# Expert gathers issued by a tile budget of 20 buffers instead of three parts ahead

## The chip, the cores and the metric

The kernel runs on one core of a Trainium2 chip. Its time is device microseconds for one execution. The engines are PE (matrix products), DVE (vector work), ACT (activations), Pool (here almost only the issue of indirect DMAs, that is, gathers and scatters by a list of rows) and SP (issue of plain DMAs). Each engine runs its own queue of instructions in order and waits on semaphores for the others. A DMA is issued by an engine and lands later; whoever needs its data waits for its landing.

## The reference, cut to what matters

A graph layer on 12500 nodes with 256 features, followed by a mixture of 64 experts, a norm over the nodes, a residual and a norm over the features. The part that the change touches is the mixture (shortened):

```python
logits = x @ Wg + bg
vals, idx = jax.lax.top_k(logits, TOP_K)          # two experts for each node
gates = jax.nn.softmax(vals, axis=-1)
...
h1 = gelu(einsum('ecd,edh->ech', h, w1) + b1)     # h: the tokens of each expert, 256 -> 512
h2 = einsum('ech,ehd->ecd', h1, w2) + b2          # 512 -> 256
y = zeros((N, D)).at[tok_s].add(g_s[:, None] * y_s)
```

So each node goes to two of 64 experts, its two results are weighted and added to the node's row. All data are float32.

## The kernel before, in words

The first two thirds of the time (to about 2620 us) sum the edges into the nodes, make each node's row `x2_d` (256 features and two gates), pick its two experts and number the tokens of each expert. The last 140 us are the two norms. Between them lies the stage of the experts.

There the 64 experts are ordered by their number of tokens, and `TOKENS` gives each place in this order its room (in units of 16 tokens). The room of one expert is cut into one or two **parts** of at most four **tiles** of 128 tokens; there are 73 parts with 219 tiles. Of 16 pairs of experts the last, partly filled tiles ("tails") share one product buffer (`pair_of_outputs`). For part q the loop does, in this order:

- `hidden(q)`: first layer on PE (L1960), gelu on ACT (L1964);
- `begin(q + AHEAD)` with `AHEAD = 3`: for a new expert, register loads that tell its number, three small copies by DVE of its token lists (`sort_slots`, L2118 and L2120), its weights by SP (`load`, L1884, 1026 KB, four buffers); then one gather by Pool for each tile of part q + 3 (`gather`, L1931) into one of 16 buffers `xg`;
- `turned(q + 1)`: PE turns the gathered tiles of the next part (L1947), DVE copies them to SBUF (L1951);
- `gates(q)` on DVE (L1975), `outputs(q)`: second layer on PE (L1983), bias and gate on DVE into one of ten buffers `yo` (L1987, L1988), and one scatter by Pool for each tile, which adds the rows to the nodes in `z_d` (`add_to_nodes`, L1993).

For the second part of a pair, `begin` comes between the scatters of the two tails.

PE and DVE follow the order that is written out here. For Pool, `in_order` ties every gather and scatter to those before it, so Pool's order is that of the code, too: gathers of part q + 3, scatters of part q, gathers of part q + 4, and so on. `landed` adds a real wait: since two experts may add to the same node, the scatters of one group (an expert) are only issued when those of the group before have landed in memory. Twelve tiles whose products were made long before ("early tiles", `add_early`, L1562) are added within this stage: `adds_at` puts such a scatter into the middle of the gathers of twelve of the parts, and it is a group of its own. From part 6 on, SP also loads `x` back (L2151) into the place of the early tiles.

Of the kernel before, what the change touches and what calls it, by code (L numbers as in the profile page):

```python
# [8 lines left out]
F32 = mybir.dt.float32  # L9
# [10 lines left out]
P = 128  # L20
# [3 lines left out]
E = 64  # L24
# [109 lines left out]
RPE = CAP // P  # L134
# [4 lines left out]
D2 = D + 2  # L139
# [5 lines left out]
def gnn_moe_kernel(  # L145
# [1726 lines left out]
    with ExitStack() as stack:  # L1872
# [3 lines left out]
        ps1 = stack.enter_context(tc.tile_pool(name="x_ps1", bufs=1, space=PSUM))  # L1876
        ps2 = stack.enter_context(tc.tile_pool(name="x_ps2", bufs=2, space=PSUM))

        REGS, YO, COLS = 4, 10, RPE - 1
        assert max(TOKENS) * TU <= COLS * P  # L1880

        def load(e):
            w = wp.tile([P, WROW], F32, name="w")
            nc.sync.dma_start(w, wpack[bass.ds(e, 1)].rearrange("a p f -> p (a f)"))  # L1884
# [35 lines left out]
        def gather(at, m, q=None):  # L1920

            xg = []
            for k in range(0, m, P):
                if k // P == -(-m // P) // 2 and q in adds_at:
                    st = add_early(adds_at[q], taken_at)
                    landed(st, f"early{adds_at[q]}")
                    in_order(st)
                r = max(WHOLE, min(P, m - k))
                k //= P
                g = two.tile([P, D2], F32, name="xg", bufs=16)  # L1930
                i = GP.indirect_dma_start(  # L1931
                    out=g[:r],
                    out_offset=None,
                    in_=x2_d,
                    in_offset=bass.IndirectOffsetOnAxis(ap=at[:r, 0, k : k + 1], axis=0),
                )
                in_order(i)
                xg.append(g[:r])
            return xg
# [139 lines left out]
        adds_at.update({large[(2 * i + 1) * len(large) // (2 * n)]: AT_ONCE + i for i in range(n)})  # L2079
        xg, given = {}, {}  # L2080

        def begin(q):
            i, b, m = parts[q]
            if i not in given:
                if i not in columns_of:
                    n = 1
                    at = order.index(i)
                    while n < REGS and order[at : at + n + 1] == [*range(i, i + n + 1)]:
                        n += 1
                    _, regs = nc.values_load_multi_w_load_instructions(  # L2090
                        exp_row[0:1, i : i + n],
                        engines=[SP],
                        min_val=0,
                        max_val=E - 1,
                        skip_runtime_bounds_check_because="exp_row is an order of the experts",
                    )
                    _, columns = nc.values_load_multi_w_load_instructions(
                        exp8_row[0:1, i : i + n],
                        engines=[DVE],
                        min_val=0,  # L2100
                        max_val=(E - 1) * RPE + 1,
                        skip_runtime_bounds_check_because="exp8_row is an order of the experts",
                    )
                    for k in range(n):
                        columns_of[i + k], reg_of[i + k] = columns[k], regs[k]
                sort_slots(i, 0)
                if q >= AHEAD:
                    sort_slots(i, 1)
                given[i] = load(reg_of[i])
            xg[q] = gather(table(q), m, q)  # L2110

        columns_of, reg_of = {}, {}

        def sort_slots(i, which):

            to = slice(i * RPE, i * RPE + COLS)
            of = bass.ds(columns_of[i], COLS)
            V.tensor_copy(sorted_[:, which, to], slot[:, which, of])  # L2118
# [14 lines left out]
        kept = {}  # L2133
        snd_sorted = one.tile([P, NSLOT], F32)
        with tc.manual_schedule(engines={mybir.EngineType.PE, DVE}):
            for q in range(AHEAD):
                begin(q)
            V.scalar_tensor_tensor(free, node, 0.0, spread, op0=ALU.is_equal, op1=ALU.mult)
            V.tensor_tensor(slot[:, 1], free, slot[:, 0], op=ALU.add)
            for i in sorted({parts[q][0] for q in range(AHEAD)}):  # L2140
                sort_slots(i, 1)
            xT = turned(0)
            for q, (i, b, m) in enumerate(parts):
# [6 lines left out]
                    r = rows(t0)  # L2150
                    nc.sync.dma_start(xs[:r, t0 : t0 + n], part_of(x, t0, n))  # L2151
# [246 lines left out]
```

## Time and profile before

| | us |
|---|---|
| median of three runs | 3597.57 |
| lowest and highest of them | 3569.35 and 3601.11 |
| the profiled execution's own time | 3578.71 |
| its span, first to last instruction | 3576.9 |

| engine | busy us (share of the span) |
|---|---|
| PE | 2494.7 (70%) |
| DVE | 1797.0 (50%) |
| ACT | 826.2 (23%) |
| Pool | 2186.7 (61%) |

The granted clock of PE is 0.82 of full speed in the mean over the span. In a timeline, each line has the start (us from the span's start), the duration, engine, line of the code, operation, what it writes and reads, a count, and in brackets how long the engine had been idle before it and what ended this. That releaser is inferred: where the engine named had long been done, it was another, often a DMA. A gather or scatter is busy on Pool only while it is issued; its landing is later. The table has shares over stages with different limits; what the change is worth is to be read from the experts' stage.

### The profile page before, as it was taken

What the parts mean: (1) busy time and instruction counts of PE and PEld (TensorE: products, weight loads), DVE (VectorE), ACT (ScalarE), POOL (GpSimd) and SP (SyncE); (2) the same over time, 40 slices, a digit from 0 to 9 for tenths busy, and PEclk for the clock granted to TensorE, in tenths of its full rate; (3) what the DMA queues carried; (4) which work ended last, traced back from release to release, by engine and by line L of the source; (5) the groups of instructions that cost most, each with busy time, mean ns of one, the idle gap of its engine ahead of it and who ended that gap; (6) DMA issues with size and microseconds to landing.
All of it is one profiled execution on the core that took longest, in us unless ns stands there. A gap on an engine that the chain in (4) does not pass through costs nothing. (4 is left out here: it accounts for less than half of the span.)

```text
span 3576.9 us, 40976 instructions
## 1 busy us (share of the span) xinstructions
PE 2494.7 (70%) x12046; PEld 1898.2 (53%) x12121; DVE 1797.0 (50%) x7367; ACT 826.2 (23%) x2028; POOL 2186.7 (61%) x2169
## 2 busy tenths in 40 slices
PE   2626066566666667676676666578769999999966
PEld 1515033455555545555555455456547767767756
DVE  2829554255455555655455444356643333334347
ACT  1515301122112122121222112122112211211246
POOL 6270777666666666666665666666547777777621
PEclk6657567788787878788788787788889999999988
DMA  7370853455455554555554544445466667667764
GB/s 258 109 235 4 304 191 110 144 146 152 130 144 143 147 142 139 146 140 162 162 162 145 162 152 137 138 144 179 132 171 148 162 150 193 161 173 183 174 168 144
DMA packets 319779, 562.31 MB, mean 157 GB/s; under 512 B 47850, under 2 KB 236366, under 8 KB 308798
## 3 DMA queue, kind: packets, MB, share of 16 engines
q0 software_dynamic: 119456, 266.90, 29.4%
q1 hardware_dynamic: 186555, 279.83, 24.5%
q10 hardware_dynamic: 13539, 12.90, 1.2%
q8 instruction: 99, 1.62, 0.2%
q14 instruction: 130, 1.06, 0.1%
HBM read 455.41 MB, written 105.12 MB: 157 GB/s over the span
## 5 line engine op out<-in xcount | busy, mean ns | idle before, releaser
L962 POOL DMA_INDIRECT ring<-h_d,src_col x1416 | 1364.4, 964 | 748.1 <-issue 385.4
L976 PE MATMUL p<-ring,o 128*128 128x258 f32 x2832 | 899.3, 447 | 175.0 <-DMA ring<-h_d,src_col 97.1
L976 PEld LDWEIGHTS p<-ring,o 128*128 128x128 f32 x2832 | 594.7, 223 | 337.3 <-issue 148.0
L954 DVE TENSOR_SCALAR o<-lane,rel 128x128 f32<-128x128 f32 x1416 | 356.4, 298 | 328.6 <-remote 163.8
L1993 POOL DMA_INDIRECT z_d<-yo,tables x219 | 340.5, 1555 | 146.2 <-issue 48.9
L1983 PE MATMUL yp<-w,h 128*128 128x256 f32 (+7 forms) x1928 | 381.2, 392 | 9.4 <-DVE yo L1987 8.4
L1960 PE MATMUL hp<-xT,w 128*128 128x384 f32 (+22 forms) x1168 | 350.5, 454 | 2.0 <-DVE xT L1951 1.3
L1983 PEld LDWEIGHTS yp<-w,h 128*128 128x128 f32 (+7 forms) x1928 | 296.3, 174 | 71.3 <-issue 17.2
L1964 ACT ACTIVATE h<-hp,w 128x384 f32<-128x384 f32 (+21 forms) x292 | 159.1, 546 | 622.8 <-PE hp L1960 513.7
L1960 PEld LDWEIGHTS hp<-xT,w 128*128 128x128 f32 x1168 | 218.6, 192 | 112.3 <-issue 49.6
L1931 POOL DMA_INDIRECT xg<-x_d,tables x219 | 215.3, 983 | 77.9 <-issue 52.1
L1951 DVE COPY xT<-xtp 128x768 f32<-128x768 f32 (+20 forms) x73 | 63.6, 871 | 329.6 <-PE xtp L1947 295.5
L1755 ACT ACTIVATE again<-again,factor 128x256 f32<-128x256 f32 x180 | 82.4, 502 | 634.2 <-issue 364.3
L309 POOL DMA_INDIRECT early<-in_x,src_col x140 | 149.8, 1070 | 113.4 <-DMA early_d<-early 60.8
L1051 PE MATMUL q<-ident,s 128*128 128x128 f32 x236 | 58.8, 339 | 200.7 <-DVE tables L1738 72.8
L1010 ACT COPY s<-p 128x258 f32<-128x258 f32 x118 | 44.0, 373 | 636.8 <-remote 274.1
L1730 PE MATMUL q<-r_out,tables 128*128 128x98 f32 x360 | 70.1, 327 | 160.0 <-DVE tables L1738 59.0
L591 PE MATMUL deg<-o_hi,o_lo 128*128 128x98 bf16 x1254 | 105.8, 255 | 102.8 <-issue 66.0
L1987 DVE TENSOR_TENSOR yo<-yp,bb 128x256 f32<-128x256 f32 (+6 forms) x219 | 92.9, 424 | 162.5 <-PE yp L1983 132.4
L589 ACT ACTIVATE s_lo<-lane_b,nb 128x128 bf16<-128x128 bf16 x396 | 122.1, 388 | 201.6 <-PE deg_s L593 96.0
L1730 PEld LDWEIGHTS q<-r_out,tables 128*128 128x128 f32 x360 | 65.7, 238 | 177.3 <-issue 74.4
L1051 PEld LDWEIGHTS q<-ident,s 128*128 128x128 f32 x236 | 35.2, 171 | 234.4 <-DVE tables L1738 79.5
(428 smaller groups left out, 3853.0 us busy)
## 6 DMA issues: line engine op xcount, KB each, us to landing
w<-in_wpack SPq DMA_DIRECT2D x64, 1026.0 KB
again<-early_d SPq DMA_DIRECT2D x90, 256.0 KB
ring<-h_d,src_col POOLq DMA_INDIRECT x1416
acc<-in_wpack SPq DMA_DIRECT2D x20, 1026.0 KB
early_d<-early SPq DMA_DIRECT2D x70, 256.0 KB
tables<-h_d SPq DMA_DIRECT2D x104, 128.0 KB
acc<-acc_d SPq DMA_DIRECT2D x14, 896.0 KB
acc<-in_x SPq DMA_DIRECT2D x12, 1024.0 KB
```

The costliest lines, as they stand in the source:

```text
L309: GP.indirect_dma_start(out=t[:, c % 2], out_offset=None, in_=x, in_offset=bass.IndirectOffsetOnAxis(ap=src_col[:, MC + c : MC + c + 1], a ...
L589: S.activation(s_lo[:, i], lane_b, AF.Sign, bias=nb[:, k - k0, i : i + 1])
L591: T.matmul(deg, o_lo[:, i], o_hi[:, i], start=c + i == 0, stop=False)
L954: o_last[u] = V.tensor_scalar(o_of[u][:, j], lane, rel[:, c : c + 1], None, op0=ALU.is_equal)
L962: i = GP.indirect_dma_start(out=r[:, k, :D], out_offset=None, in_=h_d, in_offset=bass.IndirectOffsetOnAxis(ap=src_col[:, c : c + 1], axis=0),)
L976: i = T.matmul(p_of[g], o_of[v][:, n], r[:, k], start=j == 0, stop=j == GR - 1)
L1730: T.matmul(p_r[:, i], wide[:, i * P : (i + 1) * P], r_out, start=True, stop=True)
L1931: i = GP.indirect_dma_start(out=g[:r], out_offset=None, in_=x2_d, in_offset=bass.IndirectOffsetOnAxis(ap=at[:r, 0, k : k + 1], axis=0),)
L1960: T.matmul(hp[:, :m], w1[:, c, j * P : (j + 1) * P], xT[:, c, :m], start=c == 0, stop=c == 1,)
L1964: S.activation(h1[:, j, :m], hp[:, :m], AF.Gelu, bias=w[:, 2 * H + 4 * D + j : 2 * H + 4 * D + j + 1],)
L1983: T.matmul(yp, h1[:, j, a : a + r], w2[:, j], start=j == 0, stop=j == 3)
L1993: st = GP.indirect_dma_start(out=z_d, out_offset=bass.IndirectOffsetOnAxis(ap=at[:r, 1, k : k + 1], axis=0), in_=yo, in_offset=None, compu ...
```

## The change

The buffers `xg` go from 16 to 20. `begin(q)` no longer stands for one part. It keeps two counters: parts whose weights were asked for (`loaded`), still up to part q + 3, and parts whose gathers were issued (`fetched`). It issues the gathers of further parts, at most two parts in one call, as long as the tiles from part q to the new one are at most 20. The register loads (`names`) and the copies of the token lists come with whichever of the two is first. The call before the loop issues three parts, as before. The early tiles stay in the middle of the gathers of the same parts, and so are issued when these are. At the end no gathers are left from the call for part 67 on.

```diff
-        REGS, YO, COLS = 4, 10, RPE - 1
+        REGS, YO, COLS, XG = 4, 10, RPE - 1, 20
...
-                g = two.tile([P, D2], F32, name="xg", bufs=16)
+                g = two.tile([P, D2], F32, name="xg", bufs=XG)
...
+        tiles_of = [-(-m // P) for _, _, m in parts]
...
-        def begin(q):
-            i, b, m = parts[q]
-            if i not in given:
...
-                sort_slots(i, 0)
-                if q >= AHEAD:
-                    sort_slots(i, 1)
-                given[i] = load(reg_of[i])
-            xg[q] = gather(table(q), m, q)
+        loaded, fetched = [0], [0]
+
+        def names(i):
+            if i in columns_of:
+                return
...
+        def begin(q, which=1):
+
+            to = min(q + AHEAD, len(parts) - 1)
+            most = fetched[0] + 2 if which else AHEAD
+            while True:
+                p = fetched[0]
+                if loaded[0] <= to and (loaded[0] <= p or p >= most):
+                    i = parts[loaded[0]][0]
+                    names(i)
+                    if i not in given:
+                        given[i] = load(reg_of[i])
+                    loaded[0] += 1
+                elif p < min(most, len(parts)) and sum(tiles_of[max(q, 0) : p + 1]) <= XG:
+                    i, b, m = parts[p]
+                    names(i)
+                    if i not in laid:
+                        sort_slots(i, 0)
+                        if which:
+                            sort_slots(i, 1)
+                        laid.append(i)
+                    xg[p] = gather(table(p), m, p)
+                    fetched[0] += 1
+                elif loaded[0] > to:
+                    break
+                else:
+                    most = p
...
-            for q in range(AHEAD):
-                begin(q)
+            begin(-1, 0)
...
-                if q not in pair_at and q + AHEAD < len(parts):
-                    begin(q + AHEAD)
+                if q not in pair_at:
+                    begin(q)
...
                     rest = pair_of_outputs([kept.pop(pair_at[q]), mine])
-                    begin(q + AHEAD)
+                    begin(q)
```

More of the change, by code (lines that the diff above doesn't have):

```diff
@@ L2080, in gnn_moe_kernel @@
         xg, given = {}, {}
-        def begin(q):
-            i, b, m = parts[q]
-            if i not in given:
[L2085 to L2105, printed above, removed]
-                sort_slots(i, 0)
-                if q >= AHEAD:
-                    sort_slots(i, 1)
-                given[i] = load(reg_of[i])
-            xg[q] = gather(table(q), m, q)
@@ new lines, in gnn_moe_kernel @@
+        loaded, fetched = [0], [0]
+        def names(i):
+            if i in columns_of:
+                return
+            n = 1
+            at = order.index(i)
+            while n < REGS and order[at : at + n + 1] == [*range(i, i + n + 1)]:
+                n += 1
+            _, regs = nc.values_load_multi_w_load_instructions(
+                exp_row[0:1, i : i + n],
+                engines=[SP],
+                min_val=0,
+                max_val=E - 1,
+                skip_runtime_bounds_check_because="exp_row is an order of the experts",
+            )
+            _, columns = nc.values_load_multi_w_load_instructions(
+                exp8_row[0:1, i : i + n],
+                engines=[DVE],
+                min_val=0,
+                max_val=(E - 1) * RPE + 1,
+                skip_runtime_bounds_check_because="exp8_row is an order of the experts",
+            )
+            for k in range(n):
+                columns_of[i + k], reg_of[i + k] = columns[k], regs[k]
@@ L2112, in gnn_moe_kernel @@
+        laid = []
         columns_of, reg_of = {}, {}
@@ L2135, in gnn_moe_kernel @@
         with tc.manual_schedule(engines={mybir.EngineType.PE, DVE}):
-            for q in range(AHEAD):
-                begin(q)
+            begin(-1, 0)
             V.scalar_tensor_tensor(free, node, 0.0, spread, op0=ALU.is_equal, op1=ALU.mult)
             V.tensor_tensor(slot[:, 1], free, slot[:, 0], op=ALU.add)
-            for i in sorted({parts[q][0] for q in range(AHEAD)}):
+            for i in laid:
                 sort_slots(i, 1)
```

## The prediction

> **What bounds the kernel now.** I read the page first, then the stage of the experts (about 2630 to 3438 us of the span) by stretches, then who waited for whom, and last the timelines of Pool and PE side by side. The page, groups by line (busy us, mean ns of one, then idle before it and what ended it):
>
> ```profile
> span 3576.9 us, 40976 instructions
> ...
> L1993 POOL DMA_INDIRECT z_d<-yo,tables x219 | 340.5, 1555 | 146.2 <-issue 48.9 <-DVE yo L1988 36.1 <-DMA z_d<-yo,tables 25.2
> ...
> L1931 POOL DMA_INDIRECT xg<-x_d,tables x219 | 215.3, 983 | 77.9 <-issue 52.1 <-PE yp L1983 12.2 <-PE hp L1960 7.9
> ```
>
> One stretch of the stage (us, then busy us of PE, PEld, DVE, ACT, POOL) and PE's largest wait for data there:
>
> ```profile
> 3000.00:3100.00 100.00, 97.71 (x444) 72.99 (x443) 38.94 (x120) 20.28 (x36) 74.84 (x59) 0.98 0.74 176
> ```
>
> ```profile
> PE xtp L1947 <- DMA xg<-x_d,tables: 19.0, 18, 2.4
> ```
>
> PE looks like the bound, at 97.7 of 100, and it loses 19.0 us in 18 waits for gathered tokens. That is all the change can reach on PE directly. But why is a gather late that is asked for three parts (some 33 us) early? Pool, then PE, around one such wait:
>
> ```profile
> 3160.38 1.11 POOL L1931 DMA_INDIRECT xg<-x_d,tables  x1 [0.30 <-issue]
> ...
> 3164.48 0.92 POOL L1931 DMA_INDIRECT xg<-x_d,tables  x1 [0.31 <-issue]
> ```
>
> ```profile
> 3147.14 5.38 PE L1983 MATMUL yp<-w,h 128*128 128x256 f32 x24
> ...
> 3162.34 4.68 PE L1960 MATMUL hp<-xT,w 128*128 128x336 f32 x16
> 3168.51 0.44 PE L1947 MATMUL xtp<-ident,xg 128*128 128x128 f32 x2 [1.49 <-DMA xg<-x_d,tables]
> ...
> 3172.09 8.04 PE L1983 MATMUL yp<-w,h 128*128 128x256 f32 x24
> ```
>
> The four gathers of part 50 are issued between 3160.38 and 3165.40, and PE, done with part 49's first layer, wants the first at 3167.02 (3162.34 + 4.68). So Pool runs almost two parts behind the place where the code asks. Its order is fixed (scatters of a part, gathers, scatters of the next), so a late scatter makes a late gather. A scatter's own wait, late in the stage (DVE, then Pool):
>
> ```profile
> 3341.08 0.35 DVE L1988 TENSOR_SCALAR yo<-yo,gate 128x256 f32<-128x256 f32 x1
> ```
>
> ```profile
> 3344.68 1.59 POOL L1993 DMA_INDIRECT z_d<-yo,tables  x1 [0.30 <-DVE yo L1987]
> ...
> 3353.10 1.62 POOL L1993 DMA_INDIRECT z_d<-yo,tables  x1 [2.95 <-DVE gate L1975]
> ```
>
> The tile scattered at 3353.10 was ready at 3341.43, and the DVE named as releaser had long been done. What came last is the landing of the scatter that ended at 3346.27: an expert's scatters wait until those of the group before (an expert, or an early tile) have landed. From 2690 on no scatter in the trace starts within a microsecond of its tile. **Pool's chain of scatters, landings and gathers sets the pace**, and PE's waits are its echo. At the end:
>
> ```profile
> 3381.14 1.55 POOL L1993 DMA_INDIRECT z_d<-yo,tables  x1 [0.30 <-issue]
> ...
> 3387.80 1.62 POOL L1993 DMA_INDIRECT z_d<-yo,tables  x1 [1.24 <-issue]
> ...
> 3391.61 1.57 POOL L1993 DMA_INDIRECT z_d<-yo,tables  x1 [0.30 <-issue]
> 3393.49 1.02 POOL L1931 DMA_INDIRECT xg<-x_d,tables  x1 [0.30 <-PE hp L1960]
> ...
> 3401.33 1.62 POOL L1993 DMA_INDIRECT z_d<-yo,tables  x1 [4.29 <-DVE yo L1987]
> ...
> 3418.16 1.59 POOL L1993 DMA_INDIRECT z_d<-yo,tables  x1 [3.00 <-DVE gate L1975]
> ...
> 3426.67 1.55 POOL L1993 DMA_INDIRECT z_d<-yo,tables  x1 [3.19 <-DMA z_d<-yo,tables]
> ...
> 3434.97 1.55 POOL L1993 DMA_INDIRECT z_d<-yo,tables  x1 [3.04 <-DMA z_d<-yo,tables]
> 3436.83 1.42 POOL L1993 DMA_INDIRECT z_d<-yo,tables  x1 [0.30 <-issue]
> ```
>
> ```profile
> 3389.67 0.33 SPq L1884 DMA_DIRECT2D w<-in_wpack  x1
> ```
>
> With no gather behind it and no weights on the way, a landing takes 3.0 to 3.2 us. The one from 3393.18 to 3401.33 took 8.15, with a weight load issued at 3389.67. A scatter costs 1.57 + 0.30 = 1.87 us of Pool, a gather 0.98 + 0.30 = 1.28. So two gathers fit into a quiet landing for nothing, and six into the loaded one.
>
> **The change, part by part.** Its own work is the same: 219 gathers, 219 scatters, 64 loads asked for at the same places against PE, and the same copies of token lists by DVE (one of three lines of them):
>
> ```profile
> L2118 DVE COPY tables<-tables 128x7 int32 x128 | 20.5, 189 | 9.8 <-issue 5.1
> ```
>
> They come a few parts earlier; DVE is idle for 61 of 100 us, and if PE had to wait for the copies of one more expert in the first calls, that is three times 0.19 us. Four more token buffers are only space. The change adds no wait of its own: a gather is asked for when its buffers are free by the count of 20. The early tiles go out sooner, so SP's loads of x that follow them don't start later. What changes is Pool's order. I wrote both orders out from the rule of `begin` over the list of 73 parts.
>
> *First term: the start.* Pool then still waits for PE:
>
> ```profile
> 2640.87 0.96 POOL L1931 DMA_INDIRECT xg<-x_d,tables  x1 [0.51 <-DVE tables L2118]
> ...
> 2649.09 1.65 POOL L1993 DMA_INDIRECT z_d<-yo,tables  x1 [6.06 <-DVE yo L1988]
> 2651.05 1.42 POOL L1993 DMA_INDIRECT z_d<-yo,tables  x1 [0.30 <-issue]
> ...
> 2660.37 1.62 POOL L1993 DMA_INDIRECT z_d<-yo,tables  x1 [4.06 <-DVE yo L1988]
> ...
> 2672.41 1.62 POOL L1993 DMA_INDIRECT z_d<-yo,tables  x1 [2.27 <-DVE yo L1988]
> ...
> 2678.88 1.46 POOL L1993 DMA_INDIRECT z_d<-yo,tables  x1 [2.96 <-DVE yo L1988]
> ...
> 2685.55 1.57 POOL L1562 DMA_INDIRECT z_d<-acc,taken_at  x1 [3.81 <-issue]
> ...
> 2690.04 1.40 POOL L1993 DMA_INDIRECT z_d<-yo,tables  x1 [0.30 <-issue]
> ```
>
> ```profile
> 2649.95 0.33 SPq L1884 DMA_DIRECT2D w<-in_wpack  x1
> ...
> 2650.97 0.39 SPq L2151 DMA_DIRECT2D acc<-in_x  x1
> ```
>
> 19.2 us of idle (6.06 + 4.06 + 2.27 + 2.96 + 3.81). After: five gathers from 2640.87 end at 2647.3, under the first wait. Scatters of part 0 end at 2652.47 as before. Three gathers to 2656.3, then the first early tile, which must see part 0 landed: 3.0 at best, 8.15 at worst; with both loads above on the way I take 6.0, so it is issued from 2658.5 to 2660.1, two gathers to 2662.6, landed at 2663.0. Four scatters to 2670.5, four gathers to 2675.6, two scatters to 2679.3, the kept tail to 2681.1, five gathers to 2687.5. The pair's second tail starts at 2687.8 instead of 2690.04, with nine more gathers behind it (parts 7 to 10). **-2.2 - 9 x 1.28 = -13.7 us** (-16.7 at 3.0, -11.5 at 8.15).
>
> *Second term: landings laid bare.* From there on before has 73 changes of group: 3 with no gather between, 4 with one, 29 with two, 37 with more. After has 75 (two early tiles now split an expert's scatters): 10 with none, 4 with one, 28 with two, 33 with more. None occurs where `begin` finds its 20 tiles full (parts 11, 13, 35, 38) and from part 67 on, where no gathers are left. At the quiet 3.0 us a bare change costs 3.0, one with two gathers 0.44, one with more only its 0.30 of issue: 7 x 3.0 - 0.44 - 4 x 0.30 = **+19.4 us**. Loaded, each of the seven costs up to 8.15 instead of 3.0, +36 more.
>
> *Third term: the end.* With PE no longer held up by gathers, its last weight loads fall earlier against Pool, and the changes into parts 67 and 68 should be quiet. Before, the second took 8.15 and the first 5.10 (from 3382.69 to 3387.80), where three gathers alone make 3 x 1.28 + 0.30 = 4.14: -4.0 - 1.0 = **-5 us**, bounds 0 and -5.
>
> The scatter's landing is also in the Trainium skill, DMA: Bandwidth & Descriptors, section "Anatomy of one DMA — SWDGE (gpsimd) path": about 2.0 us fixed, mostly the write's receipt, plus the bytes at 436 GB/s. For 128 KB that makes an estimate of 2.3 us, under the measured 3.0. By it the seven bare changes would cost 16 us rather than 21, and the sum would be about 5 us lower. It speaks against the change all the same: the wait is a latency that only other issues hide.
>
> **Sum:** -13.7 + 19.4 - 5 = +0.7 us. The profiled execution took 3578.71 us (1.8 of it around the span), so 3579.4 by that account. The median of the runs, 3597.57, lies 18.9 us above it, and the three runs spread over 32 us: I forecast 3598. A difference under 1% (36 us) can hardly be told from none here.
>
> **The rivals.** *PE is the bound (faster).* If landings fall quiet after the shift, Pool keeps up and PE's 19.0 us go. More goes with them: the 24 matmuls at 3172.09, behind such a stall, took 8.04 us against 5.38 for the same 24 undisturbed. The Trainium skill, TensorE: Matmul & The Clock Gate, section "HAM oscillation — how this bites in real kernels", says the same, that waits for data let the array's clock fall. The 18 waits come some three to a part, six stalls; at 2.7 us at most for each, I take 11 of 16: 19 + 11 = 30 less, of which Pool's tail behind PE may keep 5: -25, so 3573. Against it: Pool's lag never closes between 2690 and the end. It decides if Pool's waits for landings shrink by over 25 us.
>
> *Bare landings under load (slower).* Running freely, PE goes ahead until its ten output buffers are full; then its steps, and with them the weight loads, are tied to Pool's landings, and loads fall on the bare changes again. From half of the seven at 8.15 (+18) and no gain at the end (+5) it is +24; with all seven +42. I price it between, +32: 3630.
>
> *Nothing moves.* Were Pool's queue so late that the earlier request changes no issue time, the time stays 3598. Against it: Pool's 19.2 us of idle at the start, which only earlier requests fill.
>
> **How the numbers follow.** Forecast 0.52 (3580 to 3615), PE-bound 0.22, bare and loaded 0.20, nothing moved 0.06. The range takes in both rivals and some of the runs' spread: 3562 to 3634. Faster by over 1% needs the first rival at its full 30 us and luck besides: 0.07. Slower by over 1% is the upper half of the second: 0.15. Within 1%: 0.78.
>
> **What would show it.** First term: gathers of parts 3 and 4 back to back before the first scatter, and little Pool idle before 2690. Forecast as a whole: PE's waits for gathers gone, Pool's lag behind PE larger (over 20 us late in the stage), waits of PE or DVE for output buffers in their place, the last scatter near 3438. Second term: gaps of 3 us on Pool into parts 11, 13, 35, 38 and 67 to 72. It is wrong if scatters start right behind their tiles after 2700 (then PE is the bound), or if those gaps are 5 to 8 us.

## The result and the profile after

The changed kernel is slower by 1.2%: a median of 3631.74 us (six runs, 3625.17 to 3641.24) against 3595.26 us for the kernel before (six runs, 3569.22 to 3601.11), a ratio of 1.0119 with a 95% interval of 1.0086 to 1.0152. The forecast of 3598 us and "no change" was wrong. The time lies just inside the range and almost on the rival "bare landings under load" (3630 us). Medians here and in the table below are over all executions, while the ratios and their intervals leave out those in a slower state of the chip.

The page and Pool's groups of the profiled execution of after (it took 3638.54 us; columns: busy us, mean ns of one, then idle just before and what ended most of it):

```profile
span 3636.4 us, 40984 instructions
```

```profile
L1993 POOL DMA_INDIRECT z_d<-yo,tables x219 | 339.4, 1550 | 183.3 <-issue 52.9 <-DVE yo L1987 43.9 <-DVE yo L1988 30.7
L1931 POOL DMA_INDIRECT xg<-x_d,tables x219 | 213.3, 974 | 77.4 <-issue 53.9 <-PE yp L1983 9.1 <-PE hp L1960 8.2
```

Pool's busy time is that of before. The idle time ahead of the scatters went from 146.2 to 183.3 us: 37.1 more, as much as the whole loss of 36.5. Ahead of the gathers it stayed (77.9 and 77.4). PE's waits in the stage of the experts of after (us, count, longest):

```profile
PE yp L1983 <- DVE yo L1987: 39.6, 21, 4.2
PE hp L1960 <- DMA w<-in_wpack: 6.5, 1, 6.5
PE xtp L1947 <- DMA xg<-x_d,tables: 2.0, 3, 1.1
```

PE's 19.0 us of waits for gathered tokens went down to 2.0, which is what more gathers ahead can do. In their place stand 39.6 us of waits for DVE, and DVE waits for free output buffers. The waits of all engines in that stage of after have the row

```profile
DVE yo L1987 <- DMA z_d<-yo,tables: 104.1, 44, 10.3
```

and before the row was

```profile
DVE yo L1987 <- DMA z_d<-yo,tables: 1.7, 2, 0.9
```

A buffer `yo` is free when its scatter has landed, so PE is now held by Pool's chain from behind. The stretch in which PE was busy for 97.71 us has 92.12:

```profile
3000.00:3100.00 100.00, 92.12 (x417) 67.72 (x416) 36.21 (x112) 18.26 (x33) 69.69 (x57) 0.97 0.70 174
```

For a ledger I followed Pool's 450 instructions of the stage, from its first gather to the end of its last scatter (2629.35 to 3438.25 us before, 2652.61 to 3497.72 after), and put each idle time over 0.5 us down to the tile, where the scatter started as soon as its tile was ready, or else to the landing of the group before.

| us of Pool in the stage | before | after | difference |
|---|---|---|---|
| busy | 575.0 | 572.1 | -2.9 |
| gaps of issue | 125.0 | 123.5 | -1.5 |
| waiting for the tile | 15.4 | 8.1 | -7.3 |
| waiting for a landing | 93.1 | 141.4 | +48.3 |
| the stage | 808.9 | 845.1 | +36.2 |

The stage of after starts 23.3 us later in this one execution. That happens ahead of the changed code; in other runs on such chips it starts between 2607 and 2660 us, with the changed kernel and without.

By the number of gathers that stand between two groups, the idle time at the change of group (whatever ended it) is:

| gathers between | before: changes, us | after: changes, us |
|---|---|---|
| none ("bare") | 3, 9.2 | 10, 47.2 |
| one | 5, 12.5 | 4, 12.2 |
| two | 30, 35.6 | 29, 45.2 |
| three and more | 38, 52.3 | 35, 48.1 |

Seven of the ten bare changes of after stood in before as well, with gathers beside them, and cost 7.7 us there. So at the same ten places (parts 11, 13, 35, 38 and 67 to 72) the idle time rose from 16.9 to 47.2 us, by 30.3; the other 12.8 of the 43.1 us lie at the covered changes. In waits for landings alone it is 31.3 of the 48.3 us at the ten places (15.9 to 47.2) and 17.0 at the covered ones (77.2 to 94.2). Two of the bare changes, into parts 11 and 13, on Pool of after (start, duration, then idle in brackets):

```profile
2784.07 1.46 POOL L1993 DMA_INDIRECT z_d<-yo,tables  x1 [0.30 <-DVE gate L1975]
2793.31 1.56 POOL L1993 DMA_INDIRECT z_d<-yo,tables  x1 [7.78 <-DVE gate L1975]
...
2805.24 0.91 POOL L1931 DMA_INDIRECT xg<-x_d,tables  x1 [0.30 <-issue]
...
2808.39 1.46 POOL L1993 DMA_INDIRECT z_d<-yo,tables  x1 [0.31 <-issue]
2815.13 1.40 POOL L1993 DMA_INDIRECT z_d<-yo,tables  x1 [5.27 <-DVE yo L1988]
```

and SP's loads of weights beside them:

```profile
2784.82 0.33 SPq L1884 DMA_DIRECT2D w<-in_wpack  x1
...
2804.38 0.33 SPq L1884 DMA_DIRECT2D w<-in_wpack  x1
```

A load is issued 0.75 us after the scatter of 2784.07 starts, and the landing is waited for during 7.78 us, with nothing of Pool's to do. Then six gathers go out in a row to 2806.15, between scatters of one expert, where nothing has to land: the cover is there, but at the wrong place. The end of the stage in after, Pool and then SP:

```profile
3443.47 1.57 POOL L1993 DMA_INDIRECT z_d<-yo,tables  x1 [0.30 <-issue]
3450.40 1.55 POOL L1993 DMA_INDIRECT z_d<-yo,tables  x1 [5.36 <-DVE yo L1988]
...
3458.67 1.55 POOL L1993 DMA_INDIRECT z_d<-yo,tables  x1 [3.00 <-DVE gate L1975]
...
3476.88 1.55 POOL L1993 DMA_INDIRECT z_d<-yo,tables  x1 [4.66 <-DMA z_d<-yo,tables]
...
3486.10 1.55 POOL L1993 DMA_INDIRECT z_d<-yo,tables  x1 [3.96 <-issue]
```

```profile
3439.98 0.33 SPq L1884 DMA_DIRECT2D w<-in_wpack  x1
```

The change into part 67 has a load under way (3439.98) and takes 5.36; the one into part 68 has none and takes 3.00. Those into 70 and 71 take 4.66 and 3.96 without any load of weights; what slows them no row shows.

### The profile page after: what moved, and what is told of

It is laid out like the page before. It is cut to its first block, busy times and chain, and to the rows that moved or that the text cites. A ratio compares the mean times of both kernels' runs of the same rounds, so it can differ in the third digit from the quotient of the medians.

```text
span 3636.4 us, 40984 instructions
## 1 busy us (share of the span) xinstructions
PE 2510.8 (69%) x12046; PEld 1909.0 (52%) x12121; DVE 1797.9 (49%) x7367; ACT 825.5 (23%) x2028; POOL 2176.6 (60%) x2169
## 5 line engine op out<-in xcount | busy, mean ns | idle before, releaser
L962 POOL DMA_INDIRECT ring<-h_d,src_col x1416 | 1361.4, 961 | 768.4 <-issue 379.2
L1993 POOL DMA_INDIRECT z_d<-yo,tables x219 | 339.4, 1550 | 183.3 <-issue 52.9
L1983 PE MATMUL yp<-w,h 128*128 128x256 f32 (+7 forms) x1928 | 387.6, 391 | 42.8 <-DVE yo L1987 39.6
L1931 POOL DMA_INDIRECT xg<-x_d,tables x219 | 213.3, 974 | 77.4 <-issue 53.9
L309 POOL DMA_INDIRECT early<-in_x,src_col x140 | 146.2, 1044 | 111.0 <-DMA early_d<-early 60.1
L1730 PE MATMUL q<-r_out,tables 128*128 128x98 f32 x360 | 70.9, 330 | 163.3 <-DVE tables L1738 55.6
L246 DVE TENSOR_TENSOR o_hi<-lane_b,hi 128x2450 bf16<-128x2450 bf16 (+1 forms) x67 | 95.2, 1420 | 158.2 <-remote 156.2
L591 PEld LDWEIGHTS <-o_lo 128*128 128x128 bf16 x1254 | 87.4, 124 | 147.7 <-issue 96.8
```

The source lines that it names most:

```text
L246: V.tensor_tensor(o.rearrange("p k (a b) -> p k a b", b=2), lane_b[:p, None, :n] .rearrange("p k (a b) -> p k a b", b=2) .to_broadcast([p, ...
L309: GP.indirect_dma_start(out=t[:, c % 2], out_offset=None, in_=x, in_offset=bass.IndirectOffsetOnAxis(ap=src_col[:, MC + c : MC + c + 1], a ...
L591: T.matmul(deg, o_lo[:, i], o_hi[:, i], start=c + i == 0, stop=False)
L962: i = GP.indirect_dma_start(out=r[:, k, :D], out_offset=None, in_=h_d, in_offset=bass.IndirectOffsetOnAxis(ap=src_col[:, c : c + 1], axis=0),)
L1931: i = GP.indirect_dma_start(out=g[:r], out_offset=None, in_=x2_d, in_offset=bass.IndirectOffsetOnAxis(ap=at[:r, 0, k : k + 1], axis=0),)
L1983: T.matmul(yp, h1[:, j, a : a + r], w2[:, j], start=j == 0, stop=j == 3)
```

## The experiments

Three theories stood against each other. **A**: the loss is the bare changes, that is, where the gathers were put. **B**: the loss comes of running ahead as such; PE goes on until the ten output buffers are full, and the stage is then tied to landings. **C**: what sets the price is the loads of weights on the way while a scatter lands; without them even the bare changes would be nearly paid for by the gain at the start. All runs, each beside the kernel before on the same chip (us; the stage, the landings and the tiles as in the ledger):

| kernel | median | before | ratio, 95% | stage | landings | tiles |
|---|---|---|---|---|---|---|
| after (result) | 3631.74 | 3595.26 | 1.0119 (1.0086 to 1.0152) | 845.1 | 141.4 | 8.1 |
| even5 | 3619.89 | 3596.22 | 1.0074 (1.0046 to 1.0102) | 836.7 | 135.0 | 4.4 |
| yo7 | 3621.93 | 3596.22 | 1.0079 (1.0050 to 1.0108) | 831.6 | 128.1 | 6.1 |
| before_two | 3573.95 | 3596.22 | 0.9933 (0.9903 to 0.9964) | 775.8 | 17.6 | 53.7 |
| after_two | 3568.15 | 3596.22 | 0.9929 (0.9899 to 0.9958) | 776.8 | 41.8 | 30.5 |
| before_noload | 3546.64 | 3591.32 | 0.9900 (0.9866 to 0.9933) | 763.8 | 14.1 | 45.6 |
| after_noload | 3549.44 | 3591.32 | 0.9879 (0.9847 to 0.9912) | 763.3 | 30.6 | 27.6 |
| before_gate1 | 3592.11 | 3591.32 | 1.0019 (0.9983 to 1.0056) | 801.4 | 56.6 | 46.2 |
| even5_gate3 | 3580.91 | 3591.32 | 0.9993 (0.9963 to 1.0024) | 799.3 | 92.3 | 5.9 |
| after_half | 3570.06 | 3593.02 | 0.9951 (0.9922 to 0.9981) | 775.6 | 55.6 | 18.9 |
| even5_half | 3558.18 | 3593.02 | 0.9918 (0.9882 to 0.9954) | 768.3 | 43.5 | 22.2 |
| before_half | 3567.41 | 3593.02 | 0.9933 (0.9902 to 0.9965) | 775.9 | 39.5 | 36.4 |
| even5_gatel | 3572.44 | 3593.02 | 0.9969 (0.9934 to 1.0005) | 784.7 | 75.1 | 6.5 |
| after_cut | 3098.38 | 3086.26 | 1.0029 (1.0007 to 1.0051) | 814.2 | 116.0 | 1.0 |
| after_gate3 | 3089.34 | 3086.26 | 1.0011 (0.9994 to 1.0028) | 804.3 | 103.1 | 2.4 |
| after_again | 3576.88 | 3552.07 | 1.0064 (1.0038 to 1.0091) | 823.2 | 121.4 | 6.2 |
| cut2 | 3578.16 | 3552.07 | 1.0074 (1.0035 to 1.0112) | 827.7 | 125.5 | 6.3 |
| gate3b | 3562.70 | 3552.07 | 1.0047 (0.9996 to 1.0097) | 807.5 | 101.9 | 4.7 |
| even5_half2 | 3523.25 | 3552.07 | 0.9894 (0.9839 to 0.9948) | 767.1 | 41.5 | 25.8 |

The ratio need not be the quotient of the two medians. The chips differ, and medians that are held against each other below come from one chip unless said otherwise; rows and sums of before and after are those of the result, from profiles whose chips may be others than those of the experiments.

### even5: one part for each call, five parts ahead

The 20 buffers stay, but the gathers of one part stand in each call again, so that bare changes return to their few places.

```diff
-                elif p < min(most, len(parts)) and sum(tiles_of[max(q, 0) : p + 1]) <= XG:
+                elif p < min(most, len(parts)) and (q < 0 or p <= q + 5):
```

> The changed kernel, but the gathers of one part are issued in each call, always up to part q + 5 (two parts in the first calls), in the same 20 buffers; nothing is left out. Theory A (Pool's landings laid bare): five changes of expert have no gather beside them instead of ten, and the four in the middle cost 7.8 + 5.3 + 6.9 + 4.2 us, so the time falls by 15 to 25 us against the changed kernel, to about 3610. Theory B (running ahead as such: late scatters fill the ten output buffers and tie PE to Pool): as far ahead, so it stays at 3632 within 8 us.

Five bare changes are left, and they cost 14.9 us instead of 47.2. Yet the changes with two, and with three and more gathers between now cost 58.8 and 64.1 us, against 45.2 and 48.1 in after. Groups of Pool, and one such change, of even5:

```profile
L1993 POOL DMA_INDIRECT z_d<-yo,tables x219 | 339.9, 1552 | 174.8 <-issue 56.9 <-DVE yo L1987 34.8 <-DMA z_d<-yo,tables 25.2
```

```profile
3229.68 1.02 POOL L1931 DMA_INDIRECT xg<-x_d,tables  x1 [0.30 <-PE yp L1983]
...
3232.28 0.91 POOL L1931 DMA_INDIRECT xg<-x_d,tables  x1 [0.30 <-issue]
3240.24 1.63 POOL L1993 DMA_INDIRECT z_d<-yo,tables  x1 [7.04 <-issue]
```

Three gathers did not cover this landing: Pool was idle for another 7.04 us. The idle time ahead of scatters falls from 183.3 to 174.8 only. SP had issued two loads of weights near it, at 3227.79 and 3231.46. A alone is not the answer. The waits move to the covered changes, and most of the loss stays.

### yo7: seven output buffers instead of ten

If running far ahead of Pool were the harm, fewer buffers should hold PE closer to Pool.

```diff
-        REGS, YO, COLS, XG = 4, 10, RPE - 1, 20
+        REGS, YO, COLS, XG = 4, 7, RPE - 1, 20
```

> The changed kernel with 7 output buffers instead of 10; nothing is left out. Theory A: Pool's chain is the same length whether PE runs ahead of it by ten or by seven tiles, so the lag of the scatters falls from about 30 to about 20 us and the time stays at 3632 within 12 us. Theory B: PE, with three tiles (some 10 us) less room, is blocked more, and the time rises by 20 us or more.

The mean time from a finished tile to its scatter fell from 26.5 to 16.1 us, so PE was held closer. The ratio, 1.0079, overlaps that of even5, and both lie a little under the 1.0119 of after, which was measured apart from them. PE's largest wait and Pool's scatters in yo7:

```profile
PE yp L1983 <- DVE yo L1987: 34.6, 16, 5.0
```

```profile
L1993 POOL DMA_INDIRECT z_d<-yo,tables x219 | 339.6, 1551 | 156.8 <-issue 56.4 <-DVE yo L1987 26.5 <-DVE yo L1988 23.9
```

With less room PE does not wait more (34.6 us against 39.6). The full buffers look like a mark of Pool's being late, not its cause. B finds no support here as the cause by itself; what may be left of it stays open (below).

### before_two, after_two: every second expert adds to another array

The scatters of experts alternate between `z_d` and a second array, and one waits only for landings in its own array. So one expert's scatters follow the other's at once. The sum of the two arrays is left out, and what the second held is missing in the output.

```diff
-                out=z_d,
+                out=(z_d, h_d)[to],
...
-                landed(st, group)
+                landed(st, group, to)
```

> The kernel before, with every second expert's scatters added to another array instead of z_d, so that an expert waits only for the expert before the last; the sums into the other array are left out of the result. Theory A: Pool's idle time for landings falls from 93 to under 25 us, PE becomes the bound, and the time falls by 25 to 40 us, to about 3560. Theory B: the kernel before has no full output buffers, so little changes: 3590 within 8 us.

> The changed kernel with the same two arrays; the sums into the other array are left out of the result. Theory A: the loss of the change goes with the waits: within 8 us of the kernel before with two arrays, or below it. Theory B: it stays 25 us or more above the kernel before with two arrays.

Scatters of before_two, and then of after_two:

```profile
L1999 POOL DMA_INDIRECT h_d<-yo,tables x111 | 172.3, 1552 | 60.9 <-DVE yo L1989 31.3 <-issue 22.9 <-DVE snd_sorted L2131 1.5
L1999 POOL DMA_INDIRECT z_d<-yo,tables x108 | 167.9, 1555 | 62.2 <-DVE yo L1989 28.6 <-issue 20.9 <-DMA z_d<-acc,taken_at 5.5
```

```profile
L1999 POOL DMA_INDIRECT h_d<-yo,tables x111 | 172.3, 1552 | 46.9 <-issue 24.1 <-DVE yo L1989 17.6 <-DVE yo L1988 1.5
L1999 POOL DMA_INDIRECT z_d<-yo,tables x108 | 167.4, 1550 | 63.8 <-DVE yo L1989 25.4 <-issue 24.7 <-DMA z_d<-acc,taken_at 4.8
```

Together 123.1 and 110.7 us ahead of scatters, and the order of after is no longer behind: 5.8 us ahead in the median, with ratios that overlap, instead of 36.5 behind. The order that the change makes loses only by the waits for landings between experts. That holds for A and for C.

### before_noload, after_noload: no loads of weights while the experts run

The first four experts' weights serve for all 64, so 60 of the 64 loads of 1026 KB (and of their small biases) are left out, and all experts but those four compute with the wrong weights.

```diff
+        first = []
...
         def load(e):
+            if len(first) >= 4 and "over" not in issued:
+                first.append(first[-4])
+                return first[-1]
...
+            first.append((w, bb))
```

> The kernel before with the weights of the first four experts used for all: the other 60 weight loads are left out (so the result is another). Theory C (the landing's price is set by weight loads under way, 2.2 us after the issue without and over 4 with one): Pool's idle for landings falls from 93 to about 30 us, PE becomes the bound, the time falls by 25 to 40 us to about 3560. If the landings' price does not come from the loads, it falls by less than 10 us.

> The changed kernel with the weights of the first four experts used for all, the other 60 loads left out. Theory C: the ten bare changes of expert cost the quiet 3.0 us each, and what is left of the change's loss is under 10 us against the kernel before without loads. If bare changes alone make the loss, it stays at 25 us or more.

This is the run that decides. The scatters of before_noload, then of after_noload:

```profile
L1999 POOL DMA_INDIRECT z_d<-yo,tables x219 | 340.1, 1553 | 113.0 <-DVE yo L1994 48.8 <-issue 45.9 <-DVE yo L1993 4.6
```

```profile
L1999 POOL DMA_INDIRECT z_d<-yo,tables x219 | 339.8, 1552 | 114.9 <-issue 51.2 <-DVE yo L1994 37.1 <-DMA z_d<-yo,tables 11.8
```

The difference of 37.1 us ahead of scatters is 1.9 without loads, and the stage is as long in both (763.8 and 763.3 us). The bare changes are all still there. Those into parts 11, 13, 35, 38, 67 and 68 on Pool of after_noload:

```profile
2778.52 1.56 POOL L1999 DMA_INDIRECT z_d<-yo,tables  x1 [2.64 <-DVE xT L1957]
...
2797.78 1.32 POOL L1999 DMA_INDIRECT z_d<-yo,tables  x1 [2.53 <-DVE yo L1994]
...
3023.79 1.56 POOL L1999 DMA_INDIRECT z_d<-yo,tables  x1 [3.00 <-DMA z_d<-yo,tables]
...
3059.61 1.55 POOL L1999 DMA_INDIRECT z_d<-yo,tables  x1 [2.89 <-DVE yo L1993]
...
3361.86 1.55 POOL L1999 DMA_INDIRECT z_d<-yo,tables  x1 [3.09 <-DVE yo L1994]
3370.08 1.55 POOL L1999 DMA_INDIRECT z_d<-yo,tables  x1 [2.95 <-DMA z_d<-yo,tables]
```

They cost 17.1 us here. In after the same six cost 7.78 + 5.27 + 6.89 + 4.17 + 5.36 + 3.00 = 32.5. The other four, into parts 69 to 72, cost more here than in after, 19.6 us against 14.7, but at three of them Pool waits for its tile and not for a landing. Quiet, the landings cost 16.5 us more in the order of after than in that of before (30.6 against 14.1), and waiting for tiles 18.0 less (27.6 against 45.6): a trade at no gain. **C holds**: with loads on the way the same order loses, without them it does not.

### before_gate1, even5_gate3, even5_gatel: loads wait for a landing

If a load on the way makes a landing long, it can be held until a landing is over. In before_gate1 a load also waits until the last scatter issued so far has landed. In even5_gate3 (even5 otherwise) it waits for the third last group of scatters, in even5_gatel for the fourth, third or second last, whichever has the longest group behind it.

```diff
+            if "over" not in issued and len(last_of) >= 1:
+                tc.add_manual_dep(i.ins, last_of[-1].ins.name, ...)
...
+                last_of.append(st)
+            last_of[-1] = st
```

> The kernel before, whose weight loads also wait until the last scatter issued so far has landed, so that a load starts when a change of expert is over; nothing is left out. Theory C: loads run beside the scatters' issue, not beside the landing that Pool waits for; landing idle 93 to about 55 us, the time falls by 15 to 30 us to about 3575. Against it: a load that comes too late for PE, or one that is still under way at the next landing: 3600 or more.

> The changed kernel with one part gathered in each call (always five ahead), whose weight loads also wait for the landing of the third last group of scatters; nothing is left out. Theory C: the covered changes, which cost 123 us of idle in the kernel with one part in each call, come down to about 70, and the time from 3620 to 3580 or less. If the loss comes from running ahead as such, it stays at 3620.

> The kernel with one part gathered in each call, five ahead, whole loads, gated by the landing before the longest of the last groups instead of always the third last; nothing is left out. Theory C: a load of some 6.5 us beside three or more scatters (5.6 us and more) is nearly over at their landing: 3575, a little under the third-last gate's 3581. If not: the same as that.

The landings in before_gate1 fell from 93.1 to 56.6 us, and the time did not move. Its scatters, and PE's largest wait:

```profile
L1999 POOL DMA_INDIRECT z_d<-yo,tables x219 | 340.2, 1554 | 141.9 <-issue 54.9 <-DVE yo L1994 49.5 <-DMA z_d<-acc,taken_at 13.8
```

```profile
PE xtp L1953 <- DMA xg<-x_d,tables: 35.9, 13, 17.8
```

What was won is given back: Pool now waits for its tiles (46.2 us instead of 15.4), and PE for gathers that are asked for only three parts ahead. With five parts ahead and a milder gate the time went from a ratio of 1.0074 (even5, another chip) to 0.9993 and 0.9969. The intervals of the three gated kernels all hold 1: with five parts ahead, holding whole loads takes the loss away and wins nothing clear. The scatters of even5_gate3:

```profile
L1999 POOL DMA_INDIRECT z_d<-yo,tables x219 | 340.0, 1553 | 148.8 <-issue 46.2 <-DMA z_d<-yo,tables 28.1 <-DVE yo L1994 21.3
```

### after_half, even5_half, before_half: loads cut in two, each half waiting for a landing

Each load becomes two of about 512 KB. With the changed kernel and with even5 the first waits for the third last group of scatters, the second for the second last; with the kernel before for the second last and the last.

```diff
-            nc.sync.dma_start(w, wpack[bass.ds(e, 1)].rearrange("a p f -> p (a f)"))
+            for cols, k in ((slice(0, 2 * H), 3), (slice(2 * H, WROW), 2)):
+                i = nc.sync.dma_start(w[:, cols], ...)
+                if "over" not in issued and len(last_of) >= k:
+                    tc.add_manual_dep(i.ins, last_of[-k].ins.name, ...)
```

> The changed kernel with each weight load cut into two DMAs of 512 KB, the first waiting for the landing of the third last group of scatters, the second for that of the second last; nothing is left out. Theory C (the loss is loads on landings): each half is over before the next landing that Pool waits for, the stage's landing idle falls from 141 to about 90 us, and the time from 3630 to about 3585. If bare changes alone make the loss, under 10 us are gained.

> The same halves in the kernel that gathers one part in each call, five ahead; nothing is left out. Theory C: below the kernel with whole loads gated (3581), about 3570, and so under the kernel before; landing idle about 65 us instead of 92. If a load's length does not matter, 3581 within 8 us.

> The same halves in the kernel before, waiting for the second last and the last group; nothing is left out. Theory C: Pool's landing idle falls to about 50 us, but PE, only three parts ahead, then waits for gathers, so the time gains 10 us at most, to about 3582; running ahead is worth something only once the loads are off the landings.

The scatters of after_half, of even5_half and of before_half:

```profile
L2002 POOL DMA_INDIRECT z_d<-yo,tables x219 | 339.7, 1551 | 127.7 <-issue 49.0 <-DVE yo L1997 24.5 <-DVE yo L1996 20.5
```

```profile
L2002 POOL DMA_INDIRECT z_d<-yo,tables x219 | 340.2, 1553 | 116.3 <-issue 52.0 <-DVE yo L1997 32.8 <-DVE yo L1996 12.5
```

```profile
L2002 POOL DMA_INDIRECT z_d<-yo,tables x219 | 340.1, 1553 | 114.6 <-issue 51.0 <-DVE yo L1997 43.2 <-DVE gate L1984 5.8
```

With the halves the order of the change is 2.7 us behind that of before (3570.06 and 3567.41) instead of 36.5, with all the data moved. That is the same finding as without loads. I expected at most 10 us from this in the kernel before; it was 0.7%, some 24 us (3593.02 to 3567.41 in the medians), with waits for landings of 39.5 us instead of 93.1: even its landings were far from quiet. even5_half is faster than both kernels, by 0.8% against before (and by 1.1% on another chip, below). It is 9.2 us ahead of before_half, but their intervals overlap, so that five parts ahead help once the landings are short is likely and not shown.

### after_cut, after_gate3, after_again, cut2, gate3b, even5_half2: which half of it acts

after_cut and cut2 are the changed kernel with the loads cut and no wait; after_gate3 and gate3b have whole loads that wait for the third last group. The first pair ran on a chip on which all kernels were faster ahead of the experts (last section), so cut2 and gate3b stand beside after_again, the changed kernel itself, and even5_half2, which is even5_half.

> The changed kernel with each weight load cut into two DMAs of 512 KB, with no wait added; nothing is left out. If it is where the load falls that matters (theory C), the two halves run back to back as the one load did: 3630 within 10 us. If a load's size in one DMA is what delays the scatters' landings, it gains as much as the halves that wait: about 3570.

> The changed kernel with whole loads that wait for the landing of the third last group; nothing is left out. Theory C: as in the kernel with one part in each call, where this gate gained 39 us and left loads that outlast a short expert's scatters: 3595 within 12 us, between the changed kernel and its halves. If only cutting helps: 3630.

> The changed kernel once more, beside the next two on one chip, since the last two runs fell on a chip on which the kernel before takes 3086 us, some 500 us less, all of it ahead of the experts' stage. On a chip like the first ones: 1.012 of the kernel before. On a chip like the last one the stage is the same work, so the loss in us should be alike (30 to 40 us, a ratio of 1.010 to 1.013); if the loss there is under 10 us, chance in the phase of loads against landings is larger than the runs so far showed.

> The changed kernel with each weight load cut in two, no wait added. Theory C (the moment of a load matters): within 10 us of the changed kernel beside it. If a load's size in one DMA matters: 30 us or more under it.

> The changed kernel with whole loads that wait for the landing of the third last group. Theory C: 25 us or more under the changed kernel beside it. If only cutting helps: within 10 us of it.

> The kernel with one part gathered in each call, five ahead, and loads in two halves that wait for landings: on another chip again 20 us or more under the kernel before (0.992 was measured on the first).

The scatters of after_again, cut2, gate3b and even5_half2, all on one chip:

```profile
L1993 POOL DMA_INDIRECT z_d<-yo,tables x219 | 339.5, 1550 | 167.8 <-issue 51.0 <-DVE yo L1987 38.5 <-DMA z_d<-yo,tables 33.4
```

```profile
L1996 POOL DMA_INDIRECT z_d<-yo,tables x219 | 339.5, 1550 | 167.2 <-issue 50.8 <-DVE yo L1990 33.3 <-DMA z_d<-yo,tables 29.8
```

```profile
L1999 POOL DMA_INDIRECT z_d<-yo,tables x219 | 339.9, 1552 | 158.8 <-issue 53.5 <-DVE yo L1994 23.8 <-DMA z_d<-acc,taken_at 21.3
```

```profile
L2002 POOL DMA_INDIRECT z_d<-yo,tables x219 | 340.3, 1554 | 115.7 <-issue 55.5 <-DVE yo L1997 37.1 <-DMA z_d<-yo,tables 9.0
```

Cutting alone does nothing that shows (3578.16 against 3576.88). Waiting alone gives 14 us in the median, less than I expected, with intervals that overlap, so it is not shown to gain. On the faster chip after_cut and after_gate3 lie 9.0 us apart, in the same order, with intervals that overlap, too. Both together, with five parts ahead, give 53.6 us (3576.88 to 3523.25). The wait needs the smaller transfer, which finds its place between two landings. That reason is argued, not shown. The loss of the changed kernel itself was 1.0064 here and 1.0119 in the result: its sign repeats, its size doesn't.

## Why the prediction was wrong

**What bounds the kernel: right.** Pool's chain sets the pace. With landings passed over or quiet, the stage shortens from 808.9 to 775.8 and 763.8 us in the order of before, and from 845.1 to 776.8 and 763.3 us in that of after. These profiles are from different chips. And PE's waits for gathers were an echo: they went, and the time grew.

**First term, -13.7 us: about half.** On Pool of after the start is

```profile
2652.61 1.01 POOL L1931 DMA_INDIRECT xg<-x_d,tables  x1 [10.92 <-issue]
...
2668.90 0.95 POOL L1931 DMA_INDIRECT xg<-x_d,tables  x1 [0.31 <-issue]
2675.06 1.62 POOL L1993 DMA_INDIRECT z_d<-yo,tables  x1 [5.21 <-DVE yo L1988]
...
2717.47 1.40 POOL L1993 DMA_INDIRECT z_d<-yo,tables  x1 [0.30 <-issue]
```

The gathers of parts 0 to 4 go out in one row, as foretold, but end at 2669.85, and Pool still waits 5.21 us for the first tile. The pair's second tail starts at 2717.47; less the 23.27 us by which the stage starts later, that is 2694.2, not 2687.8. That is 4.2 us later than in before, with the nine gathers behind it, so by the sum of the prediction +4.2 - 9 x 1.28 = -7.3; in the ledger the waits for tiles fell by 7.3 us, too. Of the 6.4 us that the tail came later than foretold, 3.9 lie in part 0's tiles (its second scatter starts 25.6 us behind the first gather, before 21.7; why, no row shows) and 1.6 in the way from there to the first early tile, 7.6 instead of 6.0.

**Second term, +19.4 us: this is the step that failed.** The count was right (10 bare changes at parts 11, 13, 35, 38 and 67 to 72), and the quiet price was, too: 2.5 to 3.1 us at the six places of after_noload shown above. But the price with loads on the way, which I had put at up to 36 us more and left to a rival with a chance of 0.20, was the rule: 5.27 to 7.78 us at four of these six in after, which the prediction had named as the sign of its being wrong. With the third term it had allowed the ten places 19.4 - 5 = 14.4 us more; their waits for landings rose by 31.3. And it put the changes that stay covered at nothing; there the waits rose by 17.0. By the trace's semaphore events the last scatter of a group lands 2.2 us (the median) after its issue ends where no load is near, and after 4.43 us (before) and 4.85 us (after) in the mean where a load (of weights or of x) was issued within the 6 us ahead or the 2 behind. That is 42 and 43 of some 77 groups.

The Trainium skill, DMA: Bandwidth & Descriptors, section "Latency and other measured facts", gives the access latency of the memory as 0.2 us on average and 2 us at high load, and says that a lighter load makes a DMA's fixed cost smaller. The two landing times agree with that in sign. The DMA packets in the trace of after show something else at work, though. From 3441 to 3445 us, ahead of the change into part 67, only packets of the queue of the load run (0.85 MB), and none of the queue of the gathers and scatters, although a scatter was issued at 3441.59 and another at 3443.47; in the next 4 us that queue moves 0.39 MB. So here the scatters' data waited until the load was nearly through. What a slower memory adds, no run here tells. The estimate of 2.3 us that the prediction drew from the same page fits the quiet landing itself (2.2 us; Pool's gap of 3.0 has some 0.8 us more, from the landing to the start of the next scatter), and no loaded one.

**Third term, -5 us: wrong in sign.** The changes into parts 67 to 72 cost 23.0 us after (5.36, 3.00, 3.01, 4.66, 3.96, 3.06) and 15.3 before. The last load did come earlier against Pool, 10.4 us ahead of the first scatter of part 67 instead of 1.9 behind it. But that put it on the landing of the change into part 67, which is bare now.

**A smaller step failed as well.** I wrote that SP's loads of x would not start later. They wait for the early tiles' scatters, and Pool now runs further behind. The rows of SP's waits, before and after:

```profile
SPq L2151 <- DMA z_d<-acc,taken_at: 27.2, 1, 27.2
```

```profile
SPq L2176 <- DMA z_d<-acc,taken_at: 74.7, 3, 34.6
```

While SP stands there the weights behind it wait too, and then four loads go out within 4.14 us, of which these are the first and the last on SP of after:

```profile
3023.86 0.12 SPq L1884 DMA_DIRECT2D w<-in_wpack  x1
...
3028.00 0.33 SPq L1884 DMA_DIRECT2D w<-in_wpack  x1
```

PE's one wait of 6.5 us for weights, quoted above, ends at 3032.07, right behind them.

**The rivals.** "PE is the bound" fell: from 2717 us on no scatter of after starts less than 7 us behind its tile. "Bare landings under load" came true in sign, time and mark (PE and DVE wait for output buffers). That it met the time is partly luck: its +32 asks for 45.7 us more at the ten places (32 + 13.7), they rose by 31.3, and the 17.0 at covered changes, for which it has no term, made up for it. Its cause is only half right: yo7 speaks against the number of output buffers as what ties loads to landings, and even5 shows that landings can cost nearly as much (135.0 us against 141.4) when half of the ten places are covered. In a ledger of the forecast against the stage, 33.9 us of the error are landings (48.3 against 19.4 - 5: 16.9 at the ten places, 17.0 at the covered changes), 6.4 are tiles (-7.3 against -13.7), and the busy time and gaps gave back 4.4.

**What stays open.** Why landings cost more at covered changes, too, once PE runs ahead (in even5 the landings of its 77 groups sum to 287.8 us, before to 260.6 for 76) isn't settled. The loads are asked for by PE's progress, so that their phase against Pool's scatters can change with every edit and chip; that this is the reason is argued, not shown. On the chip of after_again that sum was 263.5, hardly more than before, and the loss was smaller. There the ten places cost 43.1 us of waits for landings, nearly as in after (47.2), and the covered changes 78.3 instead of 94.2: the part at the covered changes did not repeat.

## What to carry to other kernels

Where one queue's chain of "issue, land, issue" sets the pace, issues of other work between two links are its cover, and moving them ahead freed nothing here. Price a bare landing with the traffic that will be on the way, not by the quiet rows at the end of a stage, and ask what sets the phase of that traffic. If the landings can't be covered, keep large loads off them: cutting loads in two and holding each half for a landing gave 0.9918, where deeper prefetch alone gave 1.0074.

## What the runs showed of the hardware that I had not expected

An add by indirect DMA of 128 rows lands in 2.2 us when quiet and in 4.4 to 4.9 us in the mean with a load of about 1 MB near it, and single changes of group waited for 7 to 8 us. Cutting the load did not change that (cut2: 4.37 us near a load), nor did timing whole loads (gate3b: 4.33 us, though at 28 groups instead of 43); halves that were timed landed among the scatters almost unfelt (after_half: 2.58 us). While a load of weights runs, the queue of the gathers and scatters moves little: in the stage of after, in the half microseconds in which the load's queue moves over 205 GB/s (199 us in sum), it moves 28 GB/s, and 75 GB/s in the others.

Chips differ by 13 to 14% for the same kernel. On one the kernel before took 3086.26 us where others took 3552 to 3596. The gain lies ahead of the experts: on Pool of after_cut, on that chip, the first gather of the stage starts at

```profile
2142.02 1.01 POOL L1934 DMA_INDIRECT xg<-x_d,tables  x1 [10.38 <-issue]
```

and not at about 2630, while its stage of the experts takes 814.2 us, much as elsewhere. In the summing of edges (L962) Pool there is idle for 442.0 us, against 768.4 in after on its chip:

```profile
L962 POOL DMA_INDIRECT ring<-h_d,src_col x1416 | 1359.5, 960 | 442.0 <-issue 387.4
```

PE's granted clock ahead of the stage was 0.84 there and 0.77 in after. The cause wasn't looked for. It is a reason to compare kernels only on one chip.
